# Token-choice experts of a four-layer MetaFormer: scales from DRAM, strided row buffers, chunk-wise choice and a new order of work

## The chip, the cores and the metric

One core of a Trainium2 chip runs the whole program: TensorE (PE, with weight loads as PEld), VectorE (DVE), ScalarE (ACT), GpSimd (POOL) and SyncE (SP), which mostly starts DMAs. The metric is the device time of one execution in microseconds; less is better. The program computes in float32 almost throughout and takes about six milliseconds.

## The reference

The input is 4 images of 128 channels by 64 x 64 pixels. Four layers follow one another, and each adds a spatial operation and then a per-token feed-forward operation to its input (involution and a recurrence; deformable convolution and experts; convolution and experts; attention and top-2 experts). A token is one pixel's 128 channels, so an image has S = 4096 tokens. The change concerns the experts of the second and third layer, where each expert chooses its tokens:

```python
def _ln_t(v, eps=1e-5):
    m = jnp.mean(v, axis=-1, keepdims=True)
    s = jnp.var(v, axis=-1, keepdims=True)
    return (v - m) / jnp.sqrt(s + eps)

# E = 64 experts, K = 8 tokens each, H = 512; x is [4, 4096, 128], layer-normed
logits = jnp.einsum('bsd,ed->bse', x, gate_w) + gate_b
probs = jax.nn.softmax(logits, axis=1)                  # over the 4096 tokens
vals, idx = jax.lax.top_k(probs.transpose(0, 2, 1), K)  # per image and expert
gathered = jnp.take_along_axis(x, flat_idx[:, :, None], axis=1)
pooled = jnp.einsum('bked,bke->bed', gathered, topv)    # weighted sum of 8 tokens
h = gelu(einsum('ebd,edh->ebh', pooled and a one, weight1))
out = einsum('ebh,eho->ebo', h and a one, weight2)
# each chosen token gets its weight times the expert's output, added in place
outputs = outputs.at[...].add(weighted)
t = t + outputs
```

## The kernel before

The state `xs` stays on chip as channels by tokens: `xs[:, b, :]` is image b with 128 channels on the partitions. A chunk is 512 tokens of one image; an image has 8 chunks (`NCH`). `expert_choice` is called twice, and works on pairs of images, p = 0 and 1, with 64 experts of the first image on partitions 0 to 63 and those of the second on 64 to 127. Inside the pool `moe_a` the engines PE, ACT, DVE and POOL run in the order in which the text emits their instructions (`manual_schedule`); SP is left to the framework's scheduler. Each engine takes its queue in order, so an instruction that waits holds those behind it.

The steps, with their helper functions:

- `stat(p, j)`: centring of chunk j of pair p. PE multiplies the chunk by a centring matrix into a bank of PSUM (`moe_pd`), ACT squares it into `moe_sq`. Every four chunks `variances` sums the squares over the channels on PE into `moe_pv`, one row for each chunk.
- `scales(p)` and `inverted(p)`: ACT takes the root, DVE the reciprocal (3.35 us): `moe_rstd` holds one over the deviation, chunk by row and token by column.
- `turn_scales(p)`: four transposes on PE and a copy on DVE bring the scales of tokens onto the partitions (`moe_turned`).
- `logits(p, c)`: the scales of one chunk have to stand on all expert partitions. PE does this with a selector matrix, `moe_own`, into a bank (`moe_rb`); ACT copies the bank to `moe_chosen`; DVE multiplies by the gate's product (`moe_pl`); ACT adds the gate's bias with an Identity.
- `rows(b, c)`: the tokens of a chunk as rows, for gathering. Four transposes on PE, an ACT copy into one of five row buffers `moe_xt`, another ACT copy of the scales into column 128, and an SP DMA to the table in DRAM. Token t*128+p of the chunk stands on partition p, slot t, so the DMA writes pieces of 144 floats. The buffer is `xts[(b * NCH + c) % len(xts)]`.
- `largest(p)`: DVE finds the eight largest of 4096 logits per expert (MAX8), their places (FIND_INDEX8), and makes row numbers of them (`moe_idx`).
- `exponentials(p, c)` and `denominators(p)`: ACT sums exp(logit - largest) per chunk; ACT and DVE make shares and totals.
- `ask(p, j)`: POOL gathers the j-th chosen token of every expert from the table with an indirect DMA.
- `pool(p)`: DVE makes a diagonal matrix of share times scale for each j, PE sums the chosen tokens, centres them, DVE copies them to `moe_pooled`.

After that comes the second stage, in which 16 groups of 4 experts are computed from weights loaded 2 MB a group; four groups are loaded at the layer's beginning, and the other loads begin when the first stage's memory is free. At its end the outputs are added to `xs`.

The order of the first stage's work is written out by hand: all 16 chunks of pair 0 centred, five of pair 1, the logits and the choice of pair 0, the other eleven chunks of pair 1 with the first rows between them, then pair 1's logits with the rows of images 0, 1 and 2 and pair 0's exponentials between them, then the choice of pair 1 beside the rows of image 3 and pair 0's asks, the exponentials of pair 1, its asks, and the pooling of both.

Of the kernel before, what the change touches and what calls it, by code (L numbers as in the profile page):

```python
# [17 lines left out]
F32 = mybir.dt.float32  # L18
BF16 = mybir.dt.bfloat16
I32 = mybir.dt.int32  # L20
U32 = mybir.dt.uint32
# [7 lines left out]
P = 128  # L29
# [1216 lines left out]
def expert_choice(net, layer):  # L1246
# [24 lines left out]
    with ExitStack() as ctx:  # L1271
        dram = ctx.enter_context(tc.tile_pool(name="moe_dram", bufs=1, space=bass.MemoryType.DRAM))
        tables = [dram.tile([2 * N, ROW], F32, name=f"moe_table{p}") for p in range(PAIRS)]
        keep = ctx.enter_context(tc.tile_pool(name="moe", bufs=1))
# [23 lines left out]
        behind = keep.tile([P, 1], F32, name="moe_behind")  # L1298
        nc.gpsimd.memset(behind[0:E], 0.0)
        nc.gpsimd.memset(behind[E:P], float(N))  # L1300
# [25 lines left out]
        with (  # L1326
# [10 lines left out]
            def stat(p, j):  # L1337

                if j == 0:
                    stats[p] = (bank("pv", "pv"), [])  # L1340
                pv, squares = stats[p]
                pd = bank("a", "pd")
                nc.tensor.matmul(pd, net.cent, net.chunk(2 * p + j // NCH, j % NCH), start=True, stop=True)
                sq = sb.tile([P, CH], F32, name="moe_sq", tag="moe_sq", bufs=5)
                nc.scalar.activation(sq, pd, AF.Square)
                squares.append(sq)
                if j % 4 == 1 and j > 4:
                    variances(p, j // 4 - 1)
# [14 lines left out]
            def scales(p):  # L1363
                variances(p, 3)
                rstd = sb.tile([P, CH], F32, name="moe_rstd", tag="moe_rstd")
                nc.scalar.activation(rstd, stats[p][0], AF.Sqrt, bias=net.eps[1e-5])
                rstds[p] = rstd
# [4 lines left out]
            def turn_scales(p):  # L1372

                pt = bank("a", "pr")
                for k in range(4):
                    nc.tensor.transpose(pt[:, k * P : (k + 1) * P], rstds[p][:, k * P : (k + 1) * P], net.ident)
                turned[p] = sb.tile([P, 2, NCH, 4], F32, name="moe_turned", tag="moe_turned")
                nc.vector.tensor_copy(
                    turned[p].rearrange("p i (a q) k -> p k q (i a)", q=4),
                    pt.rearrange("p (k q r) -> p k q r", q=4, r=32)[:, :, :, 0:4],  # L1380
                )

            def logits(p, c):
                pb, pl = bank("b", "rb"), bank("a", "pl")
                q = c % 4
                rows = slice(32 * q, 32 * q + 32)
                nc.tensor.matmul(pb, own[rows, c // 4, :], rstds[p][rows], start=True, stop=True)
                for i in range(2):
                    nc.tensor.matmul(
                        pl[i * E : (i + 1) * E], cgate, net.chunk(2 * p + i, c), start=True, stop=True  # L1390
                    )
                lg = chosen[p][:, c * CH : (c + 1) * CH]
                nc.scalar.copy(lg, pb)
                nc.vector.tensor_mul(lg, lg, pl)
                nc.scalar.activation(lg, lg, AF.Identity, bias=gbias)

            xts = [sb.tile([P, 4, ROW], F32, name=f"moe_xt{i}", bufs=1) for i in range(5)]
            for t in xts:
                nc.gpsimd.memset(t[:, :, P:ROW], 0.0)

            own = sb.tile([P, 2, 2 * E], F32, name="moe_own", bufs=1)
            for q in range(4):
                group = slice(32 * q, 32 * q + 32)
                for r in range(2):
                    for i in range(2):
                        at = 32 * q + 2 * i + r
                        nc.gpsimd.tensor_copy(
                            own[group, r, i * E : (i + 1) * E], net.ident[group, at : at + 1].to_broadcast([32, E])
                        )

            def rows(b, c):

                p, i = divmod(b, 2)
                pt = bank("b", "pt")
                for t in range(4):
                    tok = slice((4 * c + t) * P, (4 * c + t + 1) * P)
                    nc.tensor.transpose(pt[:, t * P : (t + 1) * P], net.xs[:, b, tok], net.ident)
                xt = xts[(b * NCH + c) % len(xts)]
                nc.scalar.copy(xt[:, :, 0:P], pt.rearrange("p (t d) -> p t d", d=P))
                nc.scalar.copy(xt[:, :, P], turned[p][:, i, c, :])  # L1420
                first = i * N + c * CH
                nc.sync.dma_start(tables[p][first : first + CH, :].rearrange("(t p) r -> p t r", p=P), xt)

            places, shares, asked = {}, {}, {}

            def largest(p):
                top = keep.tile([P, K], F32, name=f"moe_top{p}")
                nc.vector.max(out=top, in_=chosen[p])
                tops[p] = top
                place = sb.tile([P, K], U32, name="moe_place", tag="moe_place")  # L1430
                nc.vector.max_index(out=place, in_max=top, in_values=chosen[p])
                row = sb.tile([P, K], F32, name="moe_row", tag="moe_row")
                nc.vector.tensor_copy(row, place)
                nc.vector.tensor_scalar(row, row, behind, None, op0=ALU.add)
                places[p] = sb.tile([P, K], I32, name="moe_idx", tag="moe_idx")
                nc.vector.tensor_copy(places[p], row)
                nc.vector.tensor_scalar_mul(negs[p], top[:, 0:1], -1.0)
# [3 lines left out]
            def exponentials(p, c):  # L1441

                sq = sb.tile([P, CH], F32, name="moe_sq", tag="moe_sq", bufs=5)
# [18 lines left out]
            def pool(p):  # L1462
# [4 lines left out]
                for j in range(K):  # L1467
                    diag = sb.tile([P, P], F32, name="moe_diag", tag="moe_diag", bufs=4)
# [21 lines left out]
            for j in range(5):  # L1490
                stat(1, j)
            turn_scales(0)
            pg = bank("b", "pg")
            nc.tensor.matmul(pg[:, 0:E], net.cent, gate, start=True, stop=True)
            nc.vector.tensor_copy(cgate, pg[:, 0:E])
            for c in range(NCH):
                logits(0, c)
            largest(0)
            for j in range(5, 2 * NCH):
                stat(1, j)  # L1500
                if j % 3 == 0:
                    rows(0, j // 3 - 2)
            scales(1)
            inverted(1)
            for c in range(4, NCH):
                rows(0, c)
                exponentials(0, c - 4)
            turn_scales(1)
            for c in range(NCH):
                logits(1, c)  # L1510
                if c < 4:
                    exponentials(0, c + 4)
                for n in (2 * c, 2 * c + 1):
# [1103 lines left out]
```

## Time and profile before

| what | value |
|---|---|
| three runs | 6048.29 us median (6040.84 to 6049.94) |
| the profiled execution | 6046.03 us, of which the profile's span is 6044.2 us |
| mean granted clock of TensorE | 0.973 |
| busy, share of the span | PE 94%, DVE 72%, ACT 56%, POOL 34% |
| first stage of the experts, second layer | 2460.22 to 2583.85 us |
| first stage of the experts, third layer | 2929.38 to 3048.64 us |
| row buffer to table (`moe_table<-moe_xt`) | 64 DMAs of 288 KB, 2.8 us from issue to landing in the median |

The changed code runs in two stretches of about 120 us each, 4% of the span together. The page's shares are means over seven phases with different limits, so they say little about these stretches; they are read from windows and timelines. A stage's start is the first `moe_pd` matmul, its end the last copy to `moe_pooled`. Line numbers (L1417) are those of the kernel printed above. TensorE's float32 matmuls with 512 columns appear as two records each.

### The profile page before, as it was taken

The numbers are of one execution on the slowest core, as the hardware profiler recorded it, in microseconds if no ns is written. First come the engines' busy times: TensorE is split into PE (matmuls) and PEld (weight loads), VectorE is DVE, ScalarE is ACT, GpSimd is POOL, SyncE is SP. The second block draws the span as 40 slices with busy tenths as digits, with TensorE's granted clock in tenths as the row PEclk, the third lists the DMA queues.
The fourth block names the chain that finished last, engine by engine and source line by source line (L and its number), as shares of the span: only waits on it lengthen the run. The fifth ranks groups of instructions, "written<-read, shape, count | busy, mean of one in ns | idle before, by whom it ended". The sixth has DMA issues, their size and how long they took to land. (4 is left out here: it accounts for less than half of the span.)

```text
span 6044.2 us, 97814 instructions
## 1 busy us (share of the span) xinstructions
PE 5694.5 (94%) x39923; PEld 2247.6 (37%) x39923; DVE 4381.6 (72%) x4739; ACT 3377.4 (56%) x4224; POOL 2057.5 (34%) x2015
## 2 busy tenths in 40 slices
PE   8999999889999988879969999999999999999799
PEld 2222222446667666343333222322232223222233
DVE  6888887456767676356447788878888888888666
ACT  4444444332323322521427888888888888899421
POOL 3889897027777777200000011111111111111000
PEclk9999999989999999989989999999999999999899
DMA  6434432057777777550365566666666666666200
GB/s 215 98 79 85 94 70 47 1 156 230 215 228 220 230 218 211 166 175 0 104 249 121 130 153 147 136 130 150 149 138 130 149 145 142 130 132 132 60 25 27
DMA packets 273147, 818.40 MB, mean 135 GB/s; under 512 B 42612, under 2 KB 100232, under 8 KB 226600
## 3 DMA queue, kind: packets, MB, share of 16 engines
q0 software_dynamic: 109568, 505.75, 35.2%
q1 hardware_dynamic: 163112, 306.20, 17.6%
q8 instruction: 320, 5.24, 0.4%
q14 instruction: 147, 1.20, 0.1%
HBM read 416.71 MB, written 93.13 MB: 84 GB/s over the span
## 5 line engine op out<-in xcount | busy, mean ns | idle before, releaser
L2020 ACT ACTIVATE att_ex<-att_sc,att_shift 128x1024 f32<-128x1024 f32 x2048 | 2141.5, 1111 | 289.7 <-PE att_sc L2016 172.4
L2051 DVE TENSOR_TENSOR att_dve<-att_dve,att_ex 128x2048 f32<-128x2048 f32 x704 | 1631.5, 2317 | 160.9 <-ACT att_ex L2020 135.3
L2016 PE MATMUL att_sc<-att_q,att_k 32*128 32x512 f32 x8192 | 1290.9, 643 | 8.3 <-ACT att_ex L2020 8.3
L2032 PE MATMUL att_pv<-att_ex,att_vals 128*32 128x512 f32 x8192 | 1095.6, 606 | 0.0
L998 POOL DMA_INDIRECT dcn_g<-dcn_table,dcn_idx x896 | 851.3, 950 | 355.4 <-issue 152.9
L412 DVE SCALAR_TENSOR_TENSOR inv_prod<-inv_pk,bspan,inv_seen 128x512 f32<-128x512 f32 (+1 forms) x1120 | 774.6, 743 | 141.6 <-PE inv_pk L399 141.3
L410 POOL TENSOR_TENSOR inv_prod<-inv_seen,inv_prod 128x512 f32<-128x512 f32 (+1 forms) x672 | 837.5, 1274 | 95.5 <-ACT inv_prod L409 95.5
L2049 POOL DMA_DIRECT2D att_dma<-att_ex x224 | 192.5, 859 | 1980.1 <-ACT att_ex L2020 1707.7
L409 ACT ACTIVATE inv_prod<-inv_pk,bspan 128x512 f32<-128x512 f32 (+1 forms) x672 | 436.1, 682 | 505.2 <-PE inv_pk L399 503.8
L2016 PEld LDWEIGHTS att_sc<-att_q,att_k 32*128 32x128 f32 x8192 | 424.9, 183 | 674.8 <-issue 420.0
L1006 DVE TENSOR_TENSOR dcn_g<-dcn_g,dcn_near_w 128x1024 f32<-128x1024 f32 x448 | 538.8, 1214 | 169.8 <-DMA dcn_g<-dcn_table,dcn_idx 153.9
L399 PE MATMUL inv_pk<-inv_red,wtap 32*96 32x512 f32 (+1 forms) x3584 | 512.2, 637 | 7.4 <-DVE wtap L377 7.4
L1015 PE MATMUL dcn_pt<-ident,dcn_g 128*128 128x128 f32 x3584 | 473.6, 276 | 37.2 <-issue 16.4
L1015 PEld LDWEIGHTS dcn_pt<-ident,dcn_g 128*128 128x128 f32 x3584 | 419.3, 142 | 210.6 <-issue 125.1
L421 PE MATMUL inv_out<-inv_prod,inv_fold 96*32 96x512 f32 (+1 forms) x3584 | 478.5, 606 | 8.5 <-DVE xs L429 8.5
L2032 PEld LDWEIGHTS att_pv<-att_ex,att_vals 128*32 128x32 f32 x8192 | 161.5, 108 | 757.4 <-issue 732.2
L399 PEld LDWEIGHTS inv_pk<-inv_red,wtap 32*96 32x96 f32 (+1 forms) x3584 | 131.8, 170 | 386.7 <-DVE inv_prod L412 362.6
L1034 ACT ACTIVATE dcn_fold<-dcn_pf,dcn_turn 128x256 f32<-128x256 f32 x128 | 60.2, 473 | 365.4 <-PE dcn_pf L1030 365.4
L1120 ACT COPY dcn_st<-dcn_pt 128x512 f32<-128x512 f32 x224 | 129.9, 580 | 239.1 <-PE dcn_pt L1015 239.0
L1127 PE MATMUL dcn_out<-dcn_st,dcn_wk 128*128 128x512 f32 x448 | 236.7, 611 | 21.3 <-DVE xs L1135 21.3
L2521 PE MATMUL top_po<-top_xg,top_we 128*128 128x512 f32 x512 | 233.2, 598 | 0.0
L1054 DVE TENSOR_TENSOR dcn_square<-dcn_hx,dcn_by 128x512 f32<-128x512 f32 x192 | 130.1, 678 | 113.5 <-PE dcn_by L1040 86.2
(433 smaller groups left out, 5371.0 us busy)
## 6 DMA issues: line engine op xcount, KB each, us to landing
att_dma<-att_ex POOLq DMA_DIRECT2D x224, 1024.0 KB, 7.4
inv_seen<-inv_image SPq DMA_DIRECT2D x256, 266.0 KB, 9.1
moe_w<-in_L_ffn_weight SPq DMA_DIRECT2D x64, 1024.0 KB, 14.2
att_dma<-att_ex SPq DMA_DIRECT2D x32, 1024.0 KB, 8.6
att_dve<-att_dma POOLq DMA_DIRECT2D x32, 1024.0 KB
moe_table<-moe_xt SPq DMA_DIRECT2D x64, 288.0 KB, 2.8
dcn_table<-dcn_xt SPq DMA_DIRECT2D x32, 512.0 KB, 4.9
dcn_g<-dcn_table,dcn_idx POOLq DMA_INDIRECT x896, 3.7
```

Source lines behind the costliest of these rows:

```text
L399: nc.tensor.matmul(pk[0:m], wtap[half][rg, i, blk], red[rg, h * CH : (h + 1) * CH], start=True, stop=True)
L409: nc.scalar.activation(prod[0:m, h], pk[0:m], AF.Identity, bias=by)
L410: nc.gpsimd.tensor_mul(of, view, of)
L412: nc.vector.scalar_tensor_tensor(out=of, in0=as_shape(pk[0:m], of), scalar=by, in1=view, op0=ALU.add, op1=ALU.mult)
L421: nc.tensor.matmul(po[CR * blk : CR * (blk + 1), h, :], fold[0:m], prod[0:m, h, :], start=unit == 0, stop=unit == UNITS - 1,)
L998: nc.gpsimd.indirect_dma_start(out=g[:, t, :], out_offset=None, in_=rows, in_offset=bass.IndirectOffsetOnAxis(ap=idx[:, Q4 * c + i + t, k ...
L1006: nc.vector.tensor_mul(near, near, by)
L1015: nc.tensor.matmul(pt[0][:, (i + t) * P : (i + t + 1) * P], near[:, t, q, :], net.ident, is_transpose=True, start=i + t + q == 0, stop=i + ...
L2016: nc.tensor.matmul(pes[h // 2][:, h % 2, :], ks[r, t * P : (t + 1) * P], q[r], start=True, stop=True)
L2020: nc.scalar.activation(ex[:, 2 * two : 2 * two + 2, :], pes[two], AF.Exp, bias=shifts[g][:, two : two + 1],)
L2032: nc.tensor.matmul(block["pv"][r], vals[:, t, r], ex[:, h, :], start=t == 0, stop=t == NT - 1)
L2051: nc.vector.tensor_add(block[who], block[who], ex)
```

## The change

- **Scales.** The selector matrix `moe_own` goes. SP stores `moe_rstd` to DRAM (`moe_spread`, four DMAs a pair), and for each chunk loads one row of it into 64 partitions, twice, as `moe_by` (three buffers; chunk n+2 is asked for in chunk n). `logits` multiplies `moe_by` by `moe_pl` directly.
- **Row buffers.** A chunk's token 4p+t stands on partition p, slot t: the transposes read every fourth column, and a partition's four tokens are one piece of 576 floats in DRAM. There are four buffers for five. The scales' copy into column 128 goes from ACT to POOL.
- **Choice.** After each chunk's logits, `largest_of` takes that chunk's eight largest and their places; `largest` then works on 64 candidates, and finds the row numbers with eight comparisons against the numbers 0 to 63 (`moe_order`) times the known rows (`moe_behind`, now with an entry for each chunk and rank).
- **Order.** All centring of both pairs first, with the rows of image 0 in its second half; then pair 0's logits with the rows of images 1 and 2; then pair 1's logits with the rows of images 3 and 2 and pair 0's choice and asks; then pair 1's choice and asks; then all exponentials and both poolings.
- **Buffers.** `moe_sq` 4 for 5, `moe_rstd` 1 for 2, `moe_diag` 3 for 4. The gate's copy goes from DVE to ACT.

```diff
     with ExitStack() as ctx:
         dram = ctx.enter_context(tc.tile_pool(name="moe_dram", bufs=1, space=bass.MemoryType.DRAM))
         tables = [dram.tile([2 * N, ROW], F32, name=f"moe_table{p}") for p in range(PAIRS)]
+        spread = [dram.tile([2 * NCH, CH], F32, name=f"moe_spread{p}") for p in range(PAIRS)]
...
         totals = [keep.tile([P, 1], F32, name=f"moe_total{i}") for i in range(PAIRS)]
         cgate = keep.tile([D, E], F32, name="moe_cgate")
 
-        behind = keep.tile([P, 1], F32, name="moe_behind")
-        nc.gpsimd.memset(behind[0:E], 0.0)
-        nc.gpsimd.memset(behind[E:P], float(N))
+        behind = keep.tile([P, NCH, K], F32, name="moe_behind")
+        for c in range(NCH):
+            nc.gpsimd.memset(behind[0:E, c, :], float(c * CH))
+            nc.gpsimd.memset(behind[E:P, c, :], float(N + c * CH))
+        order = keep.tile([P, NCH * K], F32, name="moe_order")
+        for i in range(NCH * K):
+            nc.gpsimd.memset(order[:, i : i + 1], float(i))
...
                 pv, squares = stats[p]
                 pd = bank("a", "pd")
                 nc.tensor.matmul(pd, net.cent, net.chunk(2 * p + j // NCH, j % NCH), start=True, stop=True)
-                sq = sb.tile([P, CH], F32, name="moe_sq", tag="moe_sq", bufs=5)
+                sq = sb.tile([P, CH], F32, name="moe_sq", tag="moe_sq", bufs=4)
                 nc.scalar.activation(sq, pd, AF.Square)
...
 
             def scales(p):
                 variances(p, 3)
-                rstd = sb.tile([P, CH], F32, name="moe_rstd", tag="moe_rstd")
+                rstd = sb.tile([P, CH], F32, name="moe_rstd", tag="moe_rstd", bufs=1)
...
 
                 pt = bank("a", "pr")
                 for k in range(4):
-                    nc.tensor.transpose(pt[:, k * P : (k + 1) * P], rstds[p][:, k * P : (k + 1) * P], net.ident)
+                    nc.tensor.transpose(pt[:, k * P : (k + 1) * P], rstds[p][:, k:CH:4], net.ident)
...
+            ways = {}
+
+            def spread_scales(p):
+                for r in range(4):
+                    nc.sync.dma_start(spread[p][4 * r : 4 * r + 4, :], rstds[p][r:P:32])
+
+            def way(p, c):
+                by = ways[p, c] = sb.tile([P, CH], F32, name="moe_by", tag="moe_by", bufs=3)
+                for i in range(2):
+                    row = i * NCH + c
+                    nc.sync.dma_start(by[i * E : (i + 1) * E], spread[p][row : row + 1, :].to_broadcast([E, CH]))
+
             def logits(p, c):
-                pb, pl = bank("b", "rb"), bank("a", "pl")
-                q = c % 4
-                rows = slice(32 * q, 32 * q + 32)
-                nc.tensor.matmul(pb, own[rows, c // 4, :], rstds[p][rows], start=True, stop=True)
+                pl = bank("a", "pl")
                 for i in range(2):
                     nc.tensor.matmul(
                         pl[i * E : (i + 1) * E], cgate, net.chunk(2 * p + i, c), start=True, stop=True
                     )
                 lg = chosen[p][:, c * CH : (c + 1) * CH]
-                nc.scalar.copy(lg, pb)
-                nc.vector.tensor_mul(lg, lg, pl)
+                nc.vector.tensor_mul(lg, ways.pop((p, c)), pl)
                 nc.scalar.activation(lg, lg, AF.Identity, bias=gbias)
-
-            xts = [sb.tile([P, 4, ROW], F32, name=f"moe_xt{i}", bufs=1) for i in range(5)]
+                n = p * NCH + c + 2
+                if n < 2 * NCH:
+                    way(*divmod(n, NCH))
+
+            xts = [sb.tile([P, 4, ROW], F32, name=f"moe_xt{i}", bufs=1) for i in range(4)]
             for t in xts:
                 nc.gpsimd.memset(t[:, :, P:ROW], 0.0)
-
-            own = sb.tile([P, 2, 2 * E], F32, name="moe_own", bufs=1)
-            for q in range(4):
-                group = slice(32 * q, 32 * q + 32)
-                for r in range(2):
-                    for i in range(2):
-                        at = 32 * q + 2 * i + r
-                        nc.gpsimd.tensor_copy(
-                            own[group, r, i * E : (i + 1) * E], net.ident[group, at : at + 1].to_broadcast([32, E])
-                        )
 
             def rows(b, c):
 
                 p, i = divmod(b, 2)
                 pt = bank("b", "pt")
                 for t in range(4):
-                    tok = slice((4 * c + t) * P, (4 * c + t + 1) * P)
-                    nc.tensor.transpose(pt[:, t * P : (t + 1) * P], net.xs[:, b, tok], net.ident)
+                    nc.tensor.transpose(pt[:, t * P : (t + 1) * P], net.chunk(b, c)[:, t:CH:4], net.ident)
                 xt = xts[(b * NCH + c) % len(xts)]
                 nc.scalar.copy(xt[:, :, 0:P], pt.rearrange("p (t d) -> p t d", d=P))
-                nc.scalar.copy(xt[:, :, P], turned[p][:, i, c, :])
+                nc.gpsimd.tensor_copy(xt[:, :, P], turned[p][:, i, c, :])
                 first = i * N + c * CH
-                nc.sync.dma_start(tables[p][first : first + CH, :].rearrange("(t p) r -> p t r", p=P), xt)
+                nc.sync.dma_start(tables[p][first : first + CH, :].rearrange("(p t) r -> p t r", t=4), xt)
 
             places, shares, asked = {}, {}, {}
+
+            peaks = [sb.tile([P, NCH, K], F32, name=f"moe_peaks{p}", bufs=1) for p in range(PAIRS)]
+            spots = [sb.tile([P, NCH, K], U32, name=f"moe_spots{p}", bufs=1) for p in range(PAIRS)]
+
+            def largest_of(p, c):
+                lg = chosen[p][:, c * CH : (c + 1) * CH]
+                nc.vector.max(out=peaks[p][:, c, :], in_=lg)
+                nc.vector.max_index(out=spots[p][:, c, :], in_max=peaks[p][:, c, :], in_values=lg)
 
             def largest(p):
                 top = keep.tile([P, K], F32, name=f"moe_top{p}")
-                nc.vector.max(out=top, in_=chosen[p])
+                flat = peaks[p].rearrange("p c k -> p (c k)")
+                nc.vector.max(out=top, in_=flat)
                 tops[p] = top
+                nc.vector.tensor_scalar_mul(negs[p], top[:, 0:1], -1.0)
                 place = sb.tile([P, K], U32, name="moe_place", tag="moe_place")
-                nc.vector.max_index(out=place, in_max=top, in_values=chosen[p])
+                nc.vector.max_index(out=place, in_max=top, in_values=flat)
+                at = sb.tile([P, K], F32, name="moe_at", tag="moe_at")
+                nc.vector.tensor_copy(at, place)
+                known = sb.tile([P, NCH, K], F32, name="moe_known", tag="moe_known")
+                nc.vector.tensor_copy(known, spots[p])
+                nc.vector.tensor_add(known, known, behind)
+                found = sb.tile([P, CH], F32, name="moe_sq", tag="moe_sq", bufs=4)
+                found = found.rearrange("p (j k) -> p j k", j=K)
+                for j in range(K):
+                    nc.vector.scalar_tensor_tensor(
+                        out=found[:, j, :],
+                        in0=order,
+                        scalar=at[:, j : j + 1],
+                        in1=known.rearrange("p c k -> p (c k)"),
+                        op0=ALU.is_equal,
+                        op1=ALU.mult,
+                    )
                 row = sb.tile([P, K], F32, name="moe_row", tag="moe_row")
-                nc.vector.tensor_copy(row, place)
-                nc.vector.tensor_scalar(row, row, behind, None, op0=ALU.add)
+                nc.vector.tensor_reduce(row, found, AX.X, ALU.add)
                 places[p] = sb.tile([P, K], I32, name="moe_idx", tag="moe_idx")
                 nc.vector.tensor_copy(places[p], row)
-                nc.vector.tensor_scalar_mul(negs[p], top[:, 0:1], -1.0)
 
             sums = [sb.tile([P, NCH], F32, name=f"moe_sums{p}", bufs=1) for p in range(PAIRS)]
 
             def exponentials(p, c):
 
...
-                    diag = sb.tile([P, P], F32, name="moe_diag", tag="moe_diag", bufs=4)
+                    diag = sb.tile([P, P], F32, name="moe_diag", tag="moe_diag", bufs=3)
...
                 stat(0, j)
             scales(0)
             inverted(0)
-            for j in range(5):
-                stat(1, j)
-            turn_scales(0)
+            spread_scales(0)
+            for c in range(2):
+                way(0, c)
             pg = bank("b", "pg")
             nc.tensor.matmul(pg[:, 0:E], net.cent, gate, start=True, stop=True)
-            nc.vector.tensor_copy(cgate, pg[:, 0:E])
-            for c in range(NCH):
-                logits(0, c)
-            largest(0)
-            for j in range(5, 2 * NCH):
+            nc.scalar.copy(cgate, pg[:, 0:E])
+            for j in range(2 * NCH):
                 stat(1, j)
-                if j % 3 == 0:
-                    rows(0, j // 3 - 2)
+                if j == 7:
+                    turn_scales(0)
+                if j > 7:
+                    rows(0, j - 8)
             scales(1)
             inverted(1)
-            for c in range(4, NCH):
-                rows(0, c)
-                exponentials(0, c - 4)
-            turn_scales(1)
+            spread_scales(1)
+            for c in range(NCH):
+                if c == 2:
+                    turn_scales(1)
+                logits(0, c)
+                rows(1, c)
+                if c > 3:
+                    rows(2, c - 4)
+                if c > 0:
+                    largest_of(0, c - 1)
+            largest_of(0, NCH - 1)
             for c in range(NCH):
                 logits(1, c)
-                if c < 4:
-                    exponentials(0, c + 4)
-                for n in (2 * c, 2 * c + 1):
-                    rows(1 + n // NCH, n % NCH)
-            denominators(0)
+                rows(3, c)
+                if c % 2:
+                    rows(2, 4 + c // 2)
+                if c > 0:
+                    largest_of(1, c - 1)
+                if c == 1:
+                    largest(0)
+                if c > 1:
+                    ask(0, c - 2)
+            ask(0, 6)
+            ask(0, 7)
+            largest_of(1, NCH - 1)
             largest(1)
-            for c in range(NCH):
-                rows(3, c)
-                ask(0, c)
-            for c in range(NCH):
-                exponentials(1, c)
-            denominators(1)
             for j in range(K):
                 ask(1, j)
+            for p in range(PAIRS):
+                for c in range(NCH):
+                    exponentials(p, c)
+                denominators(p)
             pool(0)
 
             pg = bank("b", "pb").rearrange("p (i c) -> p i c", i=NH)
```

More of the change, by code (lines that the diff above doesn't have):

```diff
@@ L1441, in exponentials @@
             def exponentials(p, c):
-                sq = sb.tile([P, CH], F32, name="moe_sq", tag="moe_sq", bufs=5)
+                sq = sb.tile([P, CH], F32, name="moe_sq", tag="moe_sq", bufs=4)
                 lg = chosen[p][:, c * CH : (c + 1) * CH]
```

## The prediction

> **What bounds it now.** I read the page's header and chain first. The chain that ended last only follows the final expert layer back, so it says nothing about a stage in mid-program; the stages have to be read from windows. I write A for the first token-choice layer (first centring at 2460.22 us, last pooled copy ended at 2583.85: 123.6 us) and B for the second (2929.38 to 3048.64: 119.3 us). Table of windows for B; the columns are window, length, busy time of PE, PEld, DVE, ACT, POOL with counts, granted clock, DMA share, GB/s.
>
> ```profile
> 2929.00:2949.00 20.00, 19.62 (x65) 6.81 (x66) 0.33 (x1) 9.82 (x17) 4.31 (x28) 1.00 0.83 296
> 2954.00:2971.00 17.00, 17.00 (x50) 3.96 (x49) 5.47 (x9) 8.93 (x15) 0.00 (x0) 1.00 0.13 47
> 2971.00:2987.00 16.00, 16.00 (x74) 6.53 (x74) 9.66 (x8) 10.07 (x21) 0.00 (x0) 1.00 0.19 57
> 2993.00:2995.00 2.00, 2.00 (x8) 0.87 (x5) 0.69 (x1) 1.27 (x4) 0.00 (x0) 0.50 0.84 255
> 2997.00:3020.00 23.00, 21.72 (x101) 9.46 (x100) 4.88 (x8) 17.60 (x47) 5.70 (x6) 1.00 0.61 180
> 3020.00:3031.00 11.00, 4.93 (x28) 3.23 (x28) 9.56 (x7) 7.61 (x25) 1.89 (x2) 0.80 1.04 286
> 3031.00:3036.00 5.00, 0.00 (x0) 0.00 (x0) 0.03 (x1) 5.00 (x16) 0.85 (x1) 0.50 0.31 86
> 3036.00:3049.00 13.00, 9.09 (x40) 7.90 (x40) 6.88 (x25) 0.66 (x3) 6.72 (x8) 0.70 0.19 45
> 3049.00:3124.00 75.00, 57.18 (x768) 32.44 (x768) 27.23 (x45) 26.74 (x39) 0.00 (x0) 0.93 0.92 337
> ```
>
> PE is full in centring and pair 0's logits; then an ACT-DVE-PE chain; from 3020 two scans on DVE; then ACT alone (exponentials of pair 1); then pooling. The last row is the experts' stage: DMA 0.92 busy on weights, whose load behind the four early ones is issued only at 2583.59 (A), when pooling is over. So a shorter or longer stage moves all that follows one for one. Groups by form in B (line, engine, operation, output and inputs, count; then busy us and mean ns, and the idle time before them by what ended it):
>
> ```profile
> L1419 ACT COPY moe_xt<-moe_pt 128x512 f32<-128x512 f32 x32 | 18.4, 578 | 3.4 <-DMA moe_table<-moe_xt 3.4
> L1395 ACT ACTIVATE moe_chosen<-moe_chosen,moe_gbias 128x512 f32<-128x512 f32 x16 | 11.5, 722 | 13.5 <-DVE moe_chosen L1394 13.5
> L1394 DVE TENSOR_TENSOR moe_chosen<-moe_chosen,moe_pl 128x512 f32<-128x512 f32 x16 | 11.0, 687 | 34.0 <-ACT moe_chosen L1393 19.3 <-PE moe_pl L1389 14.8
> L1428 DVE MAX8 moe_top<-moe_chosen 128x8 f32<-128x4096 f32 x2 | 8.9, 4429 | 1.5 <-ACT moe_chosen L1395 1.5
> L1431 DVE FIND_INDEX8 moe_place<-moe_top,moe_chosen 128x8 uint32<-128x4096 f32 x2 | 8.8, 4420 | 0.0
> ```
>
> Two lines' own views, min/median/max ns of a weight load in transposes (L1417 reads neighbouring columns, L1560 every fourth):
>
> ```profile
> L1417 PEld LDWEIGHTS moe_pt<-ident,xs x256: 137/141/231, 2506.0 to 3027.6; 128*128 128x128 f32 x128
> L1560 PEld LDWEIGHTS moe_pt<-ident,moe_hs x128: 195/213/231, 2586.6 to 3119.0; 128*128 128x128 f32 x128
> ```
>
> The DMA issues (KB each, us from issue to landing), where `att_by` is attention's load of one row of DRAM into all partitions:
>
> ```profile
> moe_table<-moe_xt SPq DMA_DIRECT2D x64, 288.0 KB, 2.8
> att_by<-att_spread SPq DMA_DIRECT2D x32, 256.0 KB, 5.4
> ```
>
> And ACT's timeline at the end of B's row copies, where a row buffer was still being stored:
>
> ```profile
> 3025.56 0.58 ACT L1419 COPY moe_xt<-moe_pt 128x512 f32<-128x512 f32 x1 [2.06 <-DMA moe_table<-moe_xt]
> ```
>
> **Centring (times from the stage's start, B).** Pair 0: 19.25 on PE, as now. Pair 1: 19.25 again, gate .3, the turned scales .7, eight row transposes. A strided four takes .68 (L1560, 3051.31 to 3051.99), an unstrided four .43 to .53; at .67, 5.4. PE ends at 44.9; root and reciprocal 4.2 more (2986.45 to 2990.63 now): R = 49.1. Four square buffers for five: the Square that waits now idles 1.30 while PE runs without a gap, so 0; if that cover went, some .6 in each of eight groups. POOL's 78 more memsets (.15 apart, 2929.15 to 2929.30: 12 us, less 3.2 for the selectors) end 17 before the first row buffer: 0.
>
> **First loop.** Per chunk DVE has the product (.65), MAX8 and FIND_INDEX8 over 512, and a value load (.08). Both scans are unseen at 512: an eighth of 4.43 is .55; a 512-wide reduce, .686, is the nearest row in size: .7 each, so a period of 2.2 (1.8 to 2.3). PE's selector matmuls (1.05 a chunk) and ACT's bank copy (.56) are gone, so neither bounds it: SP, with two scale loads and one or two stores a chunk at .37 apart (3481.59 to 3481.96 in attention), takes 1.5 at most. Unhindered, chunk 4's Identity starts at R+8.55. At the loop's head SP has four scale stores behind the reciprocal (two took 1.19 in attention: 2.2), then two loads for chunk 2, landing 2.7 later: R+5.3 against R+3.2 wanted. In text order that costs 2.1, if SP takes those loads earlier nothing; I take 1.4: R+9.95.
>
> **The row buffers** decide. There are now four, chosen by (8b+c) mod 4, so `rows(1, c)` and `rows(2, c-4)`, adjacent in the text, share one. ACT must finish the first copy, SP store it, the store land, before the second copy, and the next Identity stands behind that in ACT's order. Landing from issue is 2.4 at least, 2.8 in the median. The period is Identity .63, copy .5, SP and landing 2.75 (two scale loads may lie ahead of the store), copy .57: 4.45 (4.1 to 5.2), twice DVE's. Three periods: chunk 7's Identity at z = R+23.3. The store's rows grow from 576 to 2304 bytes: DMA moved 286 GB/s at share 1.04 on such rows and 337 at .92 on weights, so .295 MB takes 1.07 or .81 us: up to .26 less of each landing, within the bounds. The Trainium skill's "DMA: Bandwidth & Descriptors", Specifications, calls 512 bytes enough for line rate; by that the longer rows bring nothing, and the sum stays. No row here has 2304-byte rows.
>
> **Second loop.** Next Identity z+4.4, its scans to z+6.65. The final choice for pair 0: seventeen instructions of .15 to .69 (a 64-wide operation .22 in L1562, with pointer scalars .23 to .34, the 512-wide reduce .69): 4.5 (3.5 to 5.5), to z+11.15. Five periods: product 7 ends z+22.8. `ask(0, 0)` waits for that choice on POOL, the copies of the scales (.19) and seven more asks (1.25 each) behind it; ACT's copies come later, so 0, and one ask, 1.25, if not. `rows(2, 6)` and `rows(3, 6)` share a buffer (.2), then `rows(3, 7)` and `rows(2, 7)`: last copy done at z+27.1.
>
> **Tail.** Both sets of exponentials now stand here: table load 1.28, 16 of .705, a share .2: z+39.9. The asks of pair 1 (z+31 to z+41, landed z+44) are hidden. Pooling of both pairs 11.9 (12.05 and 12.67 now, the second held up .9 by asks; three diagonals for four, while PE's .45 each paces: 0). Stage = R+23.3+51.8 = 124.2 in B, +4.9. In A the first twelve passes take 6.97 for 5.42: 125.75, +2.1. PE half-clocked in parts of the loops: +.5 each. Sum +8: 6046.03, the profiled time (span 6044.2), becomes 6054; against the median, 2.26 above it, **6056**.
>
> PE ran at .50 for some 3 us in B after 2.25 idle (windows above), 10 in A. The skill's "TensorE: Matmul & The Clock Gate", Part 1, has half clock only after an idle window near 3.4 us; by it the waits of this loop would leave the clock at full, and the +.5 would be 0.
>
> **Rivals.** (1) *The shared buffer doesn't bind*: the loops run at DVE's 2.2. z is 3 x 2.25 = 6.75 earlier, the way from z to the last copy 4.6 shorter (2.2 at its start, 2.4 at its end): 11.3 less per layer than the forecast, 6033. For: PE and ACT have slack; against: the landing of 2.4, and the 2.06 wait above. It needs landings below .6 us. (2) *The scales arrive late* (slower): three buffers, two transfers each, reissued behind the row stores. Product, Identity, copy, store issue and two issues are 2.9, so three periods hold any landing up to 3.7. At attention's median 5.4 a period is 2.77: .57 on ten chunks and 2.7 at the head is 8.4, times .8 as the buffer waits cover some, so 7 a layer: 6070. At 6.1 (256 KB at 366 GB/s, .7, on top) and nothing covered it is 11.4 a layer: 6079. For: DMA is loaded with rows and scales together; against: the first such landing in attention, unloaded, took 3.4. (3) *PE at half clock through both loops*: logits took 1.97 at half clock and two row calls 1.97 (2526.18 and 2528.08); with strided ones at 1.1 a second-loop chunk has 3.65 for 2.2. Three banks cover two of five chunks: 4.4, and 1 in the first loop, 5 a layer: 6066. For: B's .50 window; against: PE's lookahead.
>
> **Chances.** Forecast .56, own range 6046 to 6070; (1) .12; (2) .21; (3) .11. A measurement here tells some 0.2%, 12 us, from nothing. Above 6060.4 lie (2), most of (3) and a third of the forecast: .45; below 6036.2 most of (1): .13; between .42. The range leaves out one in ten a side: 6036 to 6080.
>
> **What would show it.** Right: ACT idle before the row copies, ended by the row store's landing, 2 to 3 us four times a layer in the first loop's second half, and once before the exponentials; DVE's products 2.2 apart early and 4.4 apart there; 12.8 us of exponentials before pooling; `moe_top` scans of .7. Wrong: products evenly 2.2 apart (rival 1); DVE idle until `moe_by` lands (2); clock .5 in the loops (3); scans of 512 far from .7.

## The result and the profile after

The changed kernel took 6062.21 us (median of 8 runs, 6056.75 to 6066.62), the kernel before beside it 6046.73 (8 runs): a ratio of 1.0026, 95% interval [1.0017, 1.0035]. So it is slower by a quarter of a percent; the interval leaves out 1, but not by much. A second set of runs, on another chip, gave 1.0016 [1.0007, 1.0025]. The forecast of 6056 was 6 us short, inside its own range.

The profiled execution has a span of 6059.3 us, 15.1 more than before. Measured as in the prediction, from first centring to last pooled copy, stage A went from 123.6 to 129.6 us and stage B from 119.3 to 127.6: 14.3 us, so nearly all of the difference lies in the two stages that the diff edits. What lies between and behind them moved by +5.3 and -5.7; in a second profile of the same kernel the first was +.8, and the second varies from 2989.0 to 2999.8 us among all kernels here, none of which is edited there. B's new windows (us, then busy time of PE, PEld, DVE, ACT, POOL with counts, granted clock, DMA share, GB/s):

```profile
2966.00:2984.00 18.00, 18.00 (x90) 8.77 (x88) 0.27 (x1) 10.30 (x20) 1.51 (x9) 1.00 0.52 191
2998.00:3015.00 17.00, 9.40 (x33) 3.92 (x32) 7.93 (x16) 4.85 (x9) 0.89 (x6) 0.80 0.55 186
3015.00:3043.00 28.00, 15.24 (x76) 7.94 (x76) 22.72 (x64) 13.43 (x24) 7.28 (x19) 0.93 0.61 208
3043.00:3056.00 13.00, 0.00 (x0) 0.00 (x0) 1.90 (x8) 12.97 (x36) 9.67 (x11) 0.50 0.25 74
```

Centring is PE's alone, as before. The second row is the part of the first loop where `rows(1, c)` and `rows(2, c-4)` alternate: in 17 us no engine is busy for much over half. Whatever costs time there is a wait. The last row is the tail, 13 us in which ACT is full and only POOL's asks run for long beside it; before had 5 us of ACT there.

The groups by form in B (line, engine, operation, output and inputs, count; busy us and mean ns; idle time before them by what ended it) answer to those of before:

```profile
L1424 ACT COPY moe_xt<-moe_pt 128x512 f32<-128x512 f32 x32 | 18.6, 588 | 23.0 <-DMA moe_table<-moe_xt 19.9 <-PE moe_pl L1403 3.1
L1408 ACT ACTIVATE moe_chosen<-moe_chosen,moe_gbias 128x512 f32<-128x512 f32 x16 | 11.6, 723 | 11.9 <-DVE moe_chosen L1407 11.8
L1436 DVE MAX8 moe_peaks<-moe_chosen 128x8 f32<-128x512 f32 x16 | 11.0, 690 | 9.3 <-ACT moe_chosen L1408 9.3
L1437 DVE FIND_INDEX8 moe_spots<-moe_peaks,moe_chosen 128x8 uint32<-128x512 f32 x16 | 11.0, 685 | 0.0
L1407 DVE TENSOR_TENSOR moe_chosen<-moe_by,moe_pl 128x512 f32<-128x512 f32 x16 | 10.6, 676 | 6.3 <-DMA moe_by<-moe_spread 4.2 <-PE moe_pl L1403 2.1
```

The copies into the row buffers now idle 23.0 us, 19.9 of them for a buffer's store, where they idled 3.4; the products wait 4.2 for their scales. A scan over 512 takes .69, as estimated (.7). ACT's timeline in the second window (start, duration, engine, line; in brackets the idle time before it and what ended it):

```profile
2998.99 0.56 ACT L1424 COPY moe_xt<-moe_pt 128x512 f32<-128x512 f32 x1
3003.41 0.59 ACT L1424 COPY moe_xt<-moe_pt 128x512 f32<-128x512 f32 x1 [3.86 <-DMA moe_table<-moe_xt]
3003.89 0.72 ACT L1408 ACTIVATE moe_chosen<-moe_chosen,moe_gbias 128x512 f32<-128x512 f32 x1
3004.52 0.58 ACT L1424 COPY moe_xt<-moe_pt 128x512 f32<-128x512 f32 x1
3009.91 0.59 ACT L1424 COPY moe_xt<-moe_pt 128x512 f32<-128x512 f32 x1 [4.82 <-DMA moe_table<-moe_xt]
3010.39 0.72 ACT L1408 ACTIVATE moe_chosen<-moe_chosen,moe_gbias 128x512 f32<-128x512 f32 x1
```

This is the predicted pattern: first copy into a buffer, wait until it is stored, second copy into the same buffer, and only then the next Identity, at 3003.89 and 3010.39. SP's issues from the first of these copies on (the durations of groups reach from first to last):

```profile
2999.61 0.33 SPq L1427 DMA_DIRECT2D moe_table<-moe_xt  x1
3000.03 1.73 SPq L1398 DMA_DIRECT2D moe_by<-moe_spread  x3
3004.07 0.33 SPq L1427 DMA_DIRECT2D moe_table<-moe_xt  x1
3004.45 0.44 SPq L1398 DMA_DIRECT2D moe_by<-moe_spread  x1
3005.15 0.37 SPq L1427 DMA_DIRECT2D moe_table<-moe_xt  x1
3005.62 3.77 SPq L1398 DMA_DIRECT2D moe_by<-moe_spread  x3
```

The store that the wait is for goes out at once, at 2999.61 and 3005.15, but its buffer is free only 3.8 and 4.8 us later, while scale loads are issued around it.

### The profile page after: what moved, and what is told of

It reads as the page before. It is cut to its first block, busy times and chain, and to the rows that moved or that the text cites. A ratio compares the mean times of both kernels' runs of the same rounds, so it can differ in the third digit from the quotient of the medians.

```text
span 6059.3 us, 98032 instructions
## 1 busy us (share of the span) xinstructions
PE 5672.2 (94%) x39828; PEld 2249.9 (37%) x39859; DVE 4399.8 (73%) x4873; ACT 3354.2 (55%) x4130; POOL 2071.7 (34%) x2201
## 5 line engine op out<-in xcount | busy, mean ns | idle before, releaser
L1127 PE MATMUL dcn_out<-dcn_st,dcn_wk 128*128 128x512 f32 x448 | 238.1, 614 | 23.9 <-DVE xs L1135 22.0
```

## The experiments

The kernels ran in three sets, each with the kernel before beside it on the same chip. Before took 6277 us in the first set (e1_ring, e2_exp, e3_both, e8_best), 6278 in the second (e4_ahead to e7_tail) and 6052 in the third, so times are compared by ratio; nearly all of that difference lies ahead of stage A (it starts at some 2690 us for 2461). The stage lengths come from one profile each. Those of the changed kernel, taken on both of the faster chips, are 257.2 and 258.0 together; on the slower chip neither it nor the kernel before was profiled, so stage lengths compared across chips rest on the ratios agreeing with them.

| kernel | A, us | B, us | A + B | ratio to before, 95% interval |
|---|---|---|---|---|
| before | 123.6 | 119.3 | 242.9 | 1 |
| changed, first result | 129.6 | 127.6 | 257.2 | 1.0026 [1.0017, 1.0035] |
| after_again | 129.9 | 128.1 | 258.0 | 1.0016 [1.0007, 1.0025] |
| e1_ring | 119.0 | 115.2 | 234.1 | 0.998 [0.997, 0.9989] |
| e2_exp | 129.5 | 127.5 | 257.0 | 1.0014 [1.0005, 1.0024] |
| e3_both | 116.7 | 112.7 | 229.3 | 0.997 [0.9959, 0.998] |
| e4_ahead | 132.4 | 128.1 | 260.5 | 1.0013 [1.0004, 1.0023] |
| e5_rowold | 132.3 | 127.9 | 260.2 | 1.0023 [1.0011, 1.0034] |
| e6_sel | 132.0 | 131.1 | 263.1 | 1.0031 [1.002, 1.0041] |
| e7_tail | 128.5 | 125.6 | 254.1 | 1.002 [1.001, 1.0029] |
| e8_best | 116.8 | 114.9 | 231.7 | 0.9975 [0.9966, 0.9985] |
| e9_order | 116.0 | 114.6 | 230.6 | 0.9979 [0.997, 0.9988] |
| e10_next | 109.9 | 107.6 | 217.5 | 0.9953 [0.9939, 0.9966] |

**e1_ring: does the shared buffer pace the loops?**

```diff
-                xt = xts[(b * NCH + c) % len(xts)]
+                xt = xts[len(taken) % len(xts)]
+                taken.append((b, c))
```

> The changed kernel with its four row buffers taken in the order in which rows() is called, so that two adjacent calls never share one. Theory (the shared buffer paces the loops): the waits of ACT on the row store (14 us a layer) fall below 3; chunks 4 to 7 of the first loop run 2.2 to 2.5 apart instead of 5.2; 8 to 10 us less a layer, 6038 to 6048. Rival (the scales that come by DMA, or SP's issues, pace them): the products wait for moe_by instead, at most 3 us a layer go, 6056 or more.

The stages fell by 23.9 us against after_again, 12 a layer, more than the 8 to 10 expected; the ratio is on the other side of 1. In neither layer does a row copy wait for a store any more. The same place in ACT's timeline:

```profile
3222.31 0.72 ACT L1408 ACTIVATE moe_chosen<-moe_chosen,moe_gbias 128x512 f32<-128x512 f32 x1 [0.31 <-DVE moe_chosen L1407]
3222.94 1.05 ACT L1425 COPY moe_xt<-moe_pt 128x512 f32<-128x512 f32 x2
3224.40 0.72 ACT L1408 ACTIVATE moe_chosen<-moe_chosen,moe_gbias 128x512 f32<-128x512 f32 x1 [0.41 <-DVE moe_chosen L1407]
```

The two copies of a chunk now run back to back (x2), and Identities stand 2.0 to 4.1 us apart there, where they stood 4.8 to 6.5 apart; the 2.2 to 2.5 expected was bettered twice and missed once. With four buffers and not one byte more of memory, the order in which they are handed out was worth the whole loss and 9 us on top.

**e2_exp and e3_both: what does the tail of exponentials cost?** Both move six of pair 0's chunks; e3_both has e1_ring's edit too.

```diff
                 if c > 1:
                     ask(0, c - 2)
+                    exponentials(0, c - 2)
...
-                    exponentials(p, c)
+                    if p or c > 5:
+                        exponentials(p, c)
```

> The changed kernel with six of pair 0's eight chunks of exponentials put back into the second loop, behind its row copies; buffers as in the change. Theory: ACT waits there some 9 us a layer, so six exponentials (4.2 us) fit, and 3 to 4 us a layer leave the tail: 6054 to 6057. Rival (they delay the Identities and row copies behind them by as much): 6060 to 6064.

> Both edits together, row buffers in order of use and six chunks of pair 0's exponentials in the second loop. If both act alone and add up: 12 to 14 us a layer less than the change, 6032 to 6040, faster than the kernel before. If the exponentials only filled the waits that the buffers made: as the buffers alone, within 3 us.

e2_exp left the stages where they were, 257.0; the interval of its ratio overlaps with the changed kernel's. The exponentials did not fit in for nothing: the last row copy of B ended at 103.4 us of the stage for 101.4, and pair 1's choice came 2.3 later. They did end sooner (111.2 for 114.2), but the tail did not use it: ACT's copy of pair 0's pooled sum came late in both layers,

```profile
3291.67 0.27 ACT L1508 COPY moe_raw<-moe_acc 128x128 f32<-128x128 f32 x1 [7.63 <-remote]
```

some 3 us after PE's last sum (its group ends 3288.72), and the trace names no releaser. It may be that pair 1's asks, issued until 3289.45, stood in its way; the runs do not show it. With the buffers in order, e3_both took 4.8 us less than e1_ring, 2.4 a layer where six exponentials are 4.2, and 14.3 a layer less than after_again, a little past the 12 to 14 expected. In B the last exponential ended 4.2 us earlier than in e1_ring, but from there to the stage's end it was 13.9 us for 12.2. Pair 1's eight asks (1.25 apart, from its choice on) were still being issued in that stretch; that they hold the stage's end was not tested.

**e7_tail: the same part alone, in the kernel before.**

```diff
                 rows(0, c)
-                exponentials(0, c - 4)
...
-                if c < 4:
-                    exponentials(0, c + 4)
...
+            for p in range(PAIRS):
+                for c in range(NCH):
+                    exponentials(p, c)
+                denominators(p)
```

> The kernel before with one part of the change alone, all exponentials behind the choices of both pairs. Theory (an exponential in the tail is on the path, in the loops it is not): eight exponentials more, 5.6 us a layer, less what they delay in the loops: 6052 to 6058. Rival (they delay as much in the loops of before): 6047.

The stages are 254.1 us, 11.2 more than before's on the faster chip, that is 5.6 a layer where eight exponentials of .705 are 5.6; the medians, taken side by side, differ by 9.8 us. In the order of before this part costs nearly its full length. Little comes back from the loops: the last row copy ends .8 us earlier in A and .4 in B.

**e4_ahead: are the scales late?**

```diff
-                n = p * NCH + c + 2
+                n = p * NCH + c + 3
...
-            for c in range(2):
+            for c in range(3):
                 way(0, c)
```

> The changed kernel with every pair of scale loads issued one chunk earlier (three chunks ahead for two). Theory (the shared row buffer paces, the scales are late only once or twice): 0 to 4 us less in all, 6058 to 6063. Rival (late scales pace the loops): their 7 us of waits go in each layer, 6048 or less.

The products' waits for the loads fell from 7.3 to 3.3 us over both layers, the waits of all engines for the row stores rose from 161.3 to 171.2, and the stages are 2.5 us longer than after_again's. The ratio does not tell it from the changed kernel. So the late scales, though visible, set nothing that can be told while the buffers bind.

**e10_next: and when the buffers no longer bind?** e3_both with the same edit of the loads.

> e3_both (row buffers in order of use, six chunks of exponentials in the second loop) with the scale loads issued one chunk earlier. In e3_both the products waited 14.6 us in 13 times for the loads. Theory (with the buffers out of the way the scales are what is late next, though they were not while the buffers bound): 6 to 10 us less over both layers, 219 to 224 for 229.4. Rival (earlier loads push the row stores back on SP): 229 or more.

It took 11.8 us less than e3_both in the stages, a little more than the 6 to 10 expected, where e4_ahead gained nothing: 0.9953 [0.9939, 0.9966], 6024.95 us beside 6052.24, the fastest of all here. The two ran on different chips, and the intervals of their ratios overlap; that the waits for the loads went is seen in the profiles. What the products wait for, first in e3_both, then in e10_next (us, times, both layers):

```profile
  DMA moe_by<-moe_spread: 14.6, 13
```

```profile
  DMA moe_by<-moe_spread: 3.9, 5
```

**e6_sel: the scales by PE and ACT, as before.** The selector matmul, the bank and the copy are put back, `moe_by` and its DMAs are gone; the shared buffers stay.

```diff
+                pb, pl = bank("b", "rb"), bank("a", "pl")
+                nc.tensor.matmul(pb, own[at, c // 4, :], rstds[p][at], start=True, stop=True)
...
-                nc.vector.tensor_mul(lg, ways.pop((p, c)), pl)
+                nc.scalar.copy(lg, pb)
+                nc.vector.tensor_mul(lg, lg, pl)
```

> The changed kernel with the scales spread by PE's selector matmul and ACT's copy, as before, and no scale DMAs; all else as in the change, the shared row buffers too. Theory: the first product comes 2 us earlier, SP is free for the row stores, so the shared-buffer period falls from 5.2 to about 4.3 although ACT has .56 more a chunk: 2 to 4 us a layer less, 6054 to 6058. Rival (the spread by DMA is what the change gains, as PE and ACT get 1.05 and .56 more a chunk): 6066 or more.

Slower by 5.1 us in the stages, against the expectation; the 6066 that the rival gave is where the ratio of 1.0031 leads. But it shows the price of the shared buffer by itself, without scale DMAs on SP or in the queues. The loop runs there like a clock, 5.25 us a chunk:

```profile
3227.77 0.57 ACT L1435 COPY moe_xt<-moe_pt 128x512 f32<-128x512 f32 x1
3230.56 0.59 ACT L1435 COPY moe_xt<-moe_pt 128x512 f32<-128x512 f32 x1 [2.23 <-DMA moe_table<-moe_xt]
3231.05 0.59 ACT L1410 COPY moe_chosen<-moe_rb 128x512 f32<-128x512 f32 x1
3232.39 0.72 ACT L1412 ACTIVATE moe_chosen<-moe_chosen,moe_gbias 128x512 f32<-128x512 f32 x1 [0.75 <-DVE moe_chosen L1411]
```

The wait is 2.22 to 2.24 in all eight passes of both layers. In the changed kernel's B, with scale loads around the store, it was 3.86 and 4.82, and 2.23 again in the loop's last pass (the copy at 3018.62), when no scale load was under way. So beside scale loads a store took up to 2.6 us longer to land there. The single DMA packets in the traces agree. In the changed kernel's B the last of a store's 128 packets ended 1.7 to 2.0 us after its issue when no packet of the scales was moving, and up to 4.2 us after it (the store issued at 3005.15) when some were; in e6_sel's B it ended after 1.7 to 2.3 throughout. The expectation had overlooked that ACT's bank copy and the wait for the product (.59 and .75) follow the second copy in this chain and eat what the shorter wait saves. The loss itself comes in the second loop, where most products stand 2.4 to 3.1 us apart for 2.0.

**e5_rowold: the row layout undone.** Unstrided transposes and pieces of 576 bytes.

```diff
-                    nc.tensor.transpose(pt[:, t * P : (t + 1) * P], net.chunk(b, c)[:, t:CH:4], net.ident)
+                    nc.tensor.transpose(pt[:, t * P : (t + 1) * P], net.chunk(b, c)[:, t * P : (t + 1) * P], net.ident)
...
-                nc.sync.dma_start(tables[p][first : first + CH, :].rearrange("(p t) r -> p t r", t=4), xt)
+                nc.sync.dma_start(tables[p][first : first + CH, :].rearrange("(t p) r -> p t r", p=P), xt)
```

> The changed kernel with the tokens' old place in the row buffers: unstrided row transposes, pieces of 576 bytes for 2304. Theory (the new layout matters little either way): each row call .05 us less on PE, of which eight lie on the path, each landing up to .26 longer in five waits a layer: within 3 us of 6062. Rival (the long pieces are what keeps the landings short): landings of 3.5 or more for 2.8 and 6066 or more. Other rival (strided weight loads slow PE): 6056 or less.

No difference that can be told: 2.2 us more than after_again in the stages. The two effects are both there. Weight loads of the row transposes fall from a median of 211 ns to 141, and a quiet landing takes longer. The wait of the first loop's last pass in B, with no scale load under way, in the changed kernel and in e5_rowold (A has the same 2.23 and 2.57):

```profile
3018.62 0.59 ACT L1424 COPY moe_xt<-moe_pt 128x512 f32<-128x512 f32 x1 [2.23 <-DMA moe_table<-moe_xt]
```

```profile
3233.10 0.59 ACT L1424 COPY moe_xt<-moe_pt 128x512 f32<-128x512 f32 x1 [2.57 <-DMA moe_table<-moe_xt]
```

That is .34 for 576 against 2304 bytes; the prediction allowed up to .26. The Trainium skill's "DMA: Bandwidth & Descriptors", Specifications, puts enough for line rate at 512 bytes; by that the landings would be equal. The traces show a small gain above it.

**e8_best and e9_order: another order of the same means.** Row buffers in order of use; pair 0's logits and scans stand beside the second half of pair 1's centring, twelve row calls fill the time until pair 1's scales arrive, and images 2 and 3 follow beside pair 1's logits. e8_best has pair 0's exponentials among those twelve row calls, e9_order has all exponentials in the tail.

```diff
                 stat(1, j)
...
+                if j > 7:
+                    logits(0, j - 8)
+                if j > 8:
+                    largest_of(0, j - 9)
...
+            for c in range(NCH):
+                if c < 4:
+                    rows(0, 4 + c)
+                rows(1, c)
...
+                logits(1, c)
+                rows(2, c)
+                rows(3, c)
```

> The change's means in another order: pair 0's logits and scans beside the second half of pair 1's centring, rows of images 0 and 1 with pair 0's exponentials while pair 1's scales travel, rows of images 2 and 3 beside pair 1's logits, row buffers in order of use. By the durations of the changed kernel's profile: pair 1's reciprocal done at 55 us of the stage, its first product at 64, eight chunks of 2.3 to 86, choice to 91, asks to 104, pooling to 109: 110 for 128 to 130, 6022 (6012 to 6035). Rival (what the scans cost in the loops comes back as waits of centring on DVE and ACT): 6045 or more.

> The other order of e8_best with all exponentials in the tail, behind both choices, so that ACT has only row copies while pair 1's scales travel. Theory (in e8_best ACT's exponentials, 5.6 us and a table load of 1.3, stood ahead of pair 1's first Identity, while the tail waits for the asks anyway): the first product of pair 1 comes at 65 to 66 us of the stage for 71 to 74, stages of 110 to 112 for 115 to 117; both together 222 for 231.7, ratio 0.996. Rival (the row stores of twelve chunks on four buffers hold that stretch, not the exponentials): 230 or more together, ratio 0.997 or above.

Both beat the kernel before and miss their numbers by 9 to 12 us in the two stages; by its ratio e8_best, some 6032, is still inside the range given. In e8_best the first product of pair 1 came at 71.0 us of B for 64 expected; in e9_order it came at 62.6, but the second only at 68.7, so one wait took the place of another. ACT and SP in e9_order:

```profile
2994.51 1.31 ACT L1424 COPY moe_xt<-moe_pt 128x512 f32<-128x512 f32 x2 [6.37 <-DMA moe_table<-moe_xt]
```

```profile
2986.53 2.13 SPq L1392 DMA_DIRECT2D moe_spread<-moe_rstd  x4
2988.76 2.39 SPq L1398 DMA_DIRECT2D moe_by<-moe_spread  x4
2991.25 7.04 SPq L1427 DMA_DIRECT2D moe_table<-moe_xt  x7
```

From 2986.53 to 2991.15 SP issues only scales; the row stores stand behind them, and ACT sat idle 6.37 us for a buffer. The rival named in the expectation, that the stores hold this stretch, fits this and both of its numbers.

**after_again: the control.**

> The changed kernel itself, beside the others, so that its two stages are known on the chip of the experiments (before ran 6277 there, 6047 on the first chip). Expected: the stages as on the first chip, 129.6 and 127.6 us, 257.2 together, within 3, and a ratio to before of 1.0026 within its interval. If its stages are longer there by the 3 us that one chunk's earlier loads and the old row layout seemed to cost, those two cost nothing.

As expected, 258.0. It makes e4_ahead, e5_rowold and e2_exp differ from the changed kernel by 1 to 2.5 us of 258, which one profile each does not settle.

## Why the prediction was right, point by point

- **Direction and cause.** The mechanism that decided the forecast, two adjacent row calls on one buffer, is shown by e1_ring: without it 23.9 us go. The prediction priced its absence at 11.3 us a layer (rival 1), and it measured 12.0. That these are so close is in part luck: in B the way to z is 8.4 us shorter for 6.75, and from z to the last copy 3.3 for 4.6.
- **Head.** R was +46.8 for 49.1: eight strided row calls in centring took .47 to .58 us of PE each where .67 was put, which is 1.3 of it. Chunk 4's Identity came at R+9.8 for R+9.95, but not as described: SP took chunk 2's loads ahead of the four spread stores, so product 2 did not wait and product 3 waited 1.84.
- **The mis-sized term** is the period of the shared buffer: 4.45 predicted (4.1 to 5.2), and 5.53, 6.50 and 4.80 measured in B. Of its parts, "SP and landing 2.75" failed. The bound taken from unhindered stores did not hold with scale loads in flight: ACT waited 3.86, 4.82 and 3.11 there (the trace puts the last down to a matmul), and 2.22 to 2.24 in e6_sel without them. Three periods came to 16.8 for 13.35, the largest miss.
- **Second loop and final choice.** Unhindered products were 1.99 apart for 2.2; the choice took 3.9 for 4.5; the last copy was done at z+28.0 for z+27.1. The waits at the two shared buffers there were 2.69 and 2.56; of the first the sum had only .2.
- **Tail.** Exponentials 12.9 for 12.8. Pooling 13.2 for 11.9: PE had been idle for 21.6 us, ran at a clock of .50, and its last matmuls took .80 for .49. I had taken the old rows of pooling, with PE warmer, for the new place.
- **Sum.** In B R -2.3, the way to z +3.3, from z to the pooling +1.1 and the pooling +1.3 make 127.6 of the 124.2 that was worked out (124.7 with PE's .5). A's way from R to z was 26.8, the same term too short by as much: 129.6 for 126.3. Together 6.2 us, which is what the forecast lacked. That it lacked no more is in part luck: the head, 2.3 us shorter in B than forecast, hid part of the longer wait. In the chances, "most of (1): .13" is more than the .12 that rival 1 has; nothing else rests on it.
- **Rival 2, late scales,** was visible (7.3 us of waits) and decided nothing: e4_ahead. Once the buffers no longer bind, it costs time: e10_next.
- **Rival 3, PE at half clock:** it occurs, logits at 3006.21 took 1.98 for 1.08 after idles of 2.69 and .35 us, but as a consequence of the waits. In the rows below (columns as in B's windows) the granted clock fell to .50 after 3.41 us in which PE had worked .75:

```profile
3001.40:3004.81 3.41, 0.75 (x4) 0.56 (x4) 1.16 (x3) 1.40 (x3) 0.31 (x2) 1.00 0.50 180
3004.81:3008.22 3.41, 3.04 (x8) 1.03 (x8) 1.30 (x3) 0.28 (x1) 0.00 (x0) 0.50 0.68 245
```

  The Trainium skill's "TensorE: Matmul & The Clock Gate", Part 1, with its window of some 3.4 us idle, would have left the clock at full there; the trace does not agree.
- **What the change brings otherwise.** e7_tail prices its longer tail at 11.2 us in the order of before, e1_ring its buffers at 23.9; the net loss in the stages is 14.3. If these add up, the other parts together gain some 21, which the scales by DMA (5.1 by e6_sel, with the buffers shared) and the scans chunk by chunk beside other work share; the division of the rest was not measured. That they add up is not shown either: e2_exp gained nothing by a shorter tail, and e3_both 4.8.

## What to carry to other kernels

When buffers are chosen by an index of the data, check which calls stand next to one another in the order of work: a ring counted in order of use costs nothing and was worth 24 us here. Price a store's landing with the traffic that the change itself adds, not from a quiet stretch of before. And test a second limit again after the first is gone: earlier loads were worth nothing alone and some 12 us behind the other edits, by profiles from two chips.

## What the runs showed that I had not expected

- PE fell to half clock after waits of 2.4 to 2.7 us in B's first loop; from 2998 to 3015 the granted clock was .80.
- The scale loads are dear to issue, .44 to .60 us each on SP (median .496, where the prediction took .37), against .33 for a row store of more than twice the size; sixteen per pair make SP a place where stores queue.
- ACT's 3 us of idle time behind PE's last sum in e2_exp, ended by something that the trace calls remote, stays open.
